# Attention products cut by query columns, and the value sums copied out of PSUM in one piece, in a transformer block on one core

## The chip, the cores and the metric

The kernel runs on one core of one Trainium2 chip. The metric is the device time of one execution in microseconds (us); several executions are timed and their median is given. One more execution is profiled, and everything that is said of single instructions comes from that one.

## What is computed

The input is x, 2048 tokens of 512 numbers. Cut to what matters, the reference is

```python
xn = layernorm(x)
q, k, v = split_heads(xn @ w_qkv.T)          # 16 heads of 32
scores = (q @ k.T) / sqrt(32)                # causal: later keys are masked
attn = softmax(scores) @ v
out = x + attn @ w_o.T + ffn(xn)             # ffn: gated GELU, 4096 wide, 4-bit weights
```

Everything is computed in 32-bit floats. The feed-forward weights are decoded from 4-bit codes in the kernel. The change lies in the attention alone.

## The kernel before

**Stages.** Three stages follow each other. The first (0 to 188 us) normalizes the tokens, makes the values v and the queries and keys of the first four heads, and takes the row maxima of the first two head pairs. The second (188 to 748 us) is the loop at L560 over six head pairs p = 0 to 5; a third part of the attention (748 to 875 us, L655) does the last two pairs together. Then come the output projection and the feed-forward network, to 2002 us.

**One step of the loop.** A pass over one head pair p has 40 steps, written out in `steps` (L191). The queries are taken in blocks `qb` of 512 in the order 1, 2, 3, 0 (ORDER, L71), and for each block the keys in tiles `kt` of 128, from 0 to 4·qb+3. The last four tiles of a block are the diagonal ones, whose first columns are masked away, so that they are 512, 384, 256 and 128 queries wide. This gives steps 0 to 7 for block 1, 8 to 19 for block 2, 20 to 35 for block 3 and 36 to 39 for block 0. A step does, in program order:

- on TensorE two products L281 (one for each head, h = 0 and 1) that put the negated row maxima into a PSUM bank, two products L210 that make scores of a *later* pair `ahead` for its row maxima, and two products L296 that add this pair's transposed scores to the banks of L281;
- on TensorE what `run_due` (L570) has for this step: products of probabilities with values (L344) and row sums (L355) that earlier steps put off with `later_on` (L553), which says how many steps later they run;
- on ScalarE the exponentials of both heads (L310; on a diagonal tile L316, L318 and L320, and then a select on GpSimd, L325);
- on VectorE the row maxima of the later pair (L234; L229 on the diagonal);
- `keep_attention` (L413), if a block's sums are complete, and then one quarter of a division by the row sums (`normalize_attention`, L430: a reciprocal on VectorE, a product on GpSimd), if any is left and the tile isn't a diagonal one.

Each engine works through its own instructions in this order.

**Four tiles make a group of three.** Of four key tiles off the diagonal, called a *quad* below, the first two go through `attend_pair` (L367): four products of 512 columns, two heads by two tiles, each on 32 of the 128 columns of the TensorE array, so that the four run at the same time. GpSimd adds the probabilities of tiles 0 and 1, and of 2 and 3 (`add_up`, L390), so that row sums need one product for two tiles. The third and the fourth tile go through `attend_with_rows` (L375): two products with values and two with ones, again four at a time. The pair's products run in the step of tile 3, those of the third tile in the next step, and those of the fourth two steps after that. So in four steps three have a whole set of four products and one, that of the tile with kt % 4 == 1, has none. A diagonal tile's products (`attend_diagonal`, L380) run three steps later, those of the last one two steps later, in the same step as those of the one before.

**Buffers.** The score banks of L281/L296 come from a pool of three (ps_t, also used by the transposes L262), those of L210 from another pool of three (ps_s, also used by the projections L166 of later heads, which stand in 16 of the 240 steps). The probabilities have four buffers, one for a step. Value sums and row sums have one PSUM bank each (tags m0 and m1), so the next block's first products must wait until the old sums are copied out.

**Copying out.** The value sums of even and odd tiles stand in different partitions, 0 to 63 and 64 to 127 of the bank `av`; the row sums stand in 64 to 127 of `row`. Before the change:

```python
copies[0](aT[og][qb][half], av[:64])
if p < NP - 2 and qb > 0:
    nc.vector.tensor_tensor(aT[og][qb][half], aT[og][qb][half], av[64:], ALU.add)
copies[1](sums[og, qb][half], row[64:])
```

Both copies are ScalarE's, except for p = 7.

Of the kernel before, what the change touches and what calls it, by code (L numbers as in the profile page):

```python
# [42 lines left out]
ALU = mybir.AluOpType  # L43
# [3 lines left out]
P = 128  # L47
# [3 lines left out]
D = H // HEADS  # L51
NT = S // P
TB = 512
# [3 lines left out]
NP = HEADS // 2  # L57
# [21 lines left out]
def block_kernel(  # L79
# [10 lines left out]
    nc = tc.nc  # L90
# [4 lines left out]
    def turn_tile(i, name, dtype=F32, shape=(P, TB)):  # L95
        return turns.tile(list(shape), dtype, tag=f"turn{i}", name=name)
# [5 lines left out]
    aT = [  # L102
        [late.tile([P, TB], F32, tag=f"aT{og}_{b}", name=f"aT{og}_{b}") for b in range(NTB)]
        for og in range(NOG)
    ]
# [8 lines left out]
    with (  # L114
# [42 lines left out]
        def project(og, b, which, ps=None):  # L157
            for _ in project_halves(og, b, which, ps):
                pass
# [26 lines left out]
        units, steps, first = [], [], {}  # L186
# [80 lines left out]
        def rows_when_due():  # L267
            if due and tick[0] >= due[0][0]:
                rows_from_parts()
            tick[0] += 1  # L270

        def score_cols(p, n, pool):

            qb, kt = steps[n]
            c0 = max(0, kt - 4 * qb) * P
            tiles = []
            for h in range(2):
                first = rows_of(p, h).start
                rows = slice(first, first + 3)
                ps = tile_of(pool, f"ps_t{p}_{n}_{h}")  # L280
                nc.tensor.matmul(  # L281
                    ps[:, c0:],
                    lhsT=ones_h[rows, :],
                    rhs=negs[p // 2, qb][rows, c0:],
                    start=True,
                    stop=False,
                )
                tiles.append(ps)
            return tiles
# [44 lines left out]

        avs, rows, sums = {}, {}, {}

        def add_values(p, n, prob, place, start, stop):

            qb, kt = steps[n]
            c0 = max(0, kt - 4 * qb) * P  # L340
            for h in range(2):
                head = 2 * p + h
                j = 2 * place + h
                nc.tensor.matmul(  # L344
                    avs[p, qb][D * j : D * (j + 1), c0:],
                    lhsT=v[kt // 4][:, kt % 4, D * head : D * (head + 1)],
                    rhs=prob[:, h, c0:],
                    start=start,
                    stop=stop,
                )  # L350

        def add_rows(p, qb, probs, c0, start, stop):

            for h in range(2):
                nc.tensor.matmul(  # L355
                    rows[p, qb][D * (2 + h) : D * (3 + h), c0:],
                    lhsT=ones,
                    rhs=probs[h][:, c0:],
                    start=start,
                    stop=stop,  # L360
                )

        def open_sums(p, qb):
            avs[p, qb] = ps_m.tile([P, TB], F32, tag="m0", name=f"av{p}_{qb}")
            rows[p, qb] = ps_m.tile([P, TB], F32, tag="m1", name=f"rows{p}_{qb}")

        def attend_pair(p, n, prob_a, prob_b):  # L367

            qb, kt = steps[n]
            if kt == 0:  # L370
                open_sums(p, qb)
            add_values(p, n, prob_a, 0, kt == 0, False)
            add_values(p, n + 1, prob_b, 1, kt == 0, kt == 4 * qb - 4)

        def attend_with_rows(p, n, prob, added, start):  # L375

            add_values(p, n, prob, 0, False, False)
            add_rows(p, steps[n][0], added, 0, start, False)

        def attend_diagonal(p, n, prob):  # L380
            qb, kt = steps[n]
            if kt == 0:
                open_sums(p, qb)
            last = kt == 4 * qb + 3
            add_values(p, n, prob, 0, kt == 0, last)
            add_rows(p, qb, [prob[:, h] for h in range(2)], (kt - 4 * qb) * P, kt == 0, last)
            if last:
                full.append((p, qb))

# [9 lines left out]
        def attend(p, n, prob, first, last):  # L399

            qb, kt = steps[n]
            if first:
                avs[p, qb] = ps_m.tile([P, TB], F32, tag=f"m{p % 2}", name=f"av{p}_{qb}")
                rows[p, qb] = avs[p, qb]
            add_values(p, n, prob, 0, first, last)
            c0 = max(0, kt - 4 * qb) * P
            add_rows(p, qb, [prob[:, h] for h in range(2)], c0, first, last)
            if last:
                full.append((p, qb))

# [2 lines left out]
        def keep_attention():  # L413

            p, qb = full.pop(0)
            av, row = avs[p, qb], rows[p, qb]
            og, half = p // 2, slice(64 * (p % 2), 64 * (p % 2 + 1))
            if p % 2 == 0:
                sums[og, qb] = sump.tile([P, TB], F32, tag="sums", name=f"sums{og}_{qb}")
            copies = [nc.scalar.copy] * 2  # L420
            if p == NP - 1:
                copies = [nc.vector.tensor_copy] * 2
            copies[0](aT[og][qb][half], av[:64])
            if p < NP - 2 and qb > 0:
                nc.vector.tensor_tensor(aT[og][qb][half], aT[og][qb][half], av[64:], ALU.add)
            copies[1](sums[og, qb][half], row[64:])
            if p % 2 == 1:
                invert.extend((og, qb, i) for i in range(4))

# [94 lines left out]
        for b in range(NTB):  # L524
            n = first[b]
# [27 lines left out]
        def later_on(wait, f, *args):  # L553
            todo.setdefault(at[0] + wait, []).append((f, args))

        def run_due(m):
            for f, args in todo.pop(m, []):
                f(*args)

        for m in range((NP - 2) * STEPS):  # L560
            p, n = divmod(m, STEPS)
            at[0] = m

            ahead = p + 3 if p % 2 == 0 else p + 1
            og, own = p // 2, m % (2 * STEPS)
            rows_when_due()
            ps = score_cols(p, n, ps_t)
            ps_max = score_rows(ahead, n, ps_s)
            add_scores(p, n, ps)
            run_due(m)  # L570
            prob = exponentials(p, n, ps)
            maxima(ahead, n, ps_max)
            while full:
                keep_attention()
            qb, kt = steps[n]


            if kt >= 4 * qb:
                later_on(2 if kt == 4 * qb + 3 else 3, attend_diagonal, p, n, prob)
            elif kt % 2 == 0:  # L580
                even = prob
            else:
                added = add_up(2 * quads + kt % 4 // 2, even, prob)
                if kt % 4 == 1:
                    later_on(2, attend_pair, p, n - 1, even, prob)
                    added_first = added
                else:
                    later_on(1, attend_with_rows, p, n - 1, even, added_first, kt == 3)
                    later_on(3, attend_with_rows, p, n, prob, added, False)
                    quads += 1  # L590
            if invert and kt < 4 * qb:
                normalize_attention()

            if own in places and og + 2 < NOG:
                b, which = places[own]
                project(og + 2, b, which, tile_of(ps_s, f"ps_qk{og + 2}_{b}_{which}"))
            if own in places_own and og > 0 and og + 1 < NOG:
                b, which = places_own[own]
                project(og + 1, b, which, tile_of(ps_s, f"ps_qk{og + 1}_{b}_{which}"))
            if og + 2 < NOG and own == 20:  # L600
                wqk[og + 2] = load_qk(og + 2)
            if og + 2 == NOG and own == max(places_own) + 1:

                wo = []
                for i in range(0, NOG, 2):
                    t = wa.tile([P, 2, H], F32, tag="wqk", name=f"wo{i}")
                    for k in range(2):
                        nc.sync.dma_start(out=t[:, k], in_=w_o[i + k])
                        wo.append(t[:, k])
# [45 lines left out]
        for s, n in enumerate(together):  # L655
# [6 lines left out]
            while pending:  # L662
                attend(*pending.pop(0))
            qb = steps[n][0]
# [4 lines left out]
            for i in range(2):  # L669
                prob = exponentials_together(NP - 2 + i, n, two[i])  # L670
# [135 lines left out]
    for n in range(NG * NC):  # L806
        g, j = divmod(n + 1, NC)
        pieces += [(g, 0, j), (g, 1, j)] if g < NG else [None, None]
        g, j = divmod(2 * (n // 2 + 1) + n % 2, NC)
# [48 lines left out]
    with tc.manual_schedule():  # L858
# [13 lines left out]
        for n, t in enumerate(order):  # L872
            po = bank(f"po{t}")
            for og in range(NOG):
# [3 lines left out]
                    rhs=wo[og],  # L878
                    start=(og == 0),
                    stop=(og == NOG - 1),  # L880
# [187 lines left out]
```

## Time and profile before

| | us |
|---|---|
| median of 3 runs (2004.05 to 2007.36) | 2006.99 |
| profiled execution, its own time | 2004.01 |
| its span, from the first to the last instruction | 2002.3 |
| the loop at L560, within the span | 188.1 to 747.8 |
| reciprocal L434 (VectorE, 128x128), mean of 40 in the loop | 0.944 |
| copies L423 and L426 (ScalarE, 64x512), mean of 23 each in the loop | 0.575, 0.582 |
| addition L425 (VectorE, 64x512), mean of 18 | 0.691 |

Times of single instructions are from start to end; the next instruction of the same engine can begin a little before the end. One product of 32-bit floats is two records in the trace. In a timeline, each line has the start, the length, engine, line, operation, what it writes and reads, the shape and how many records are merged; in brackets stands how long the engine was idle before it and which instruction ended that. In a table of windows, each line has the stretch and its length, then the busy time of TensorE, of its weight loads (PEld), of VectorE (DVE), ScalarE (ACT) and GpSimd (POOL), each with a count of instructions, then the granted TensorE clock as a share, and the DMA share and rate.

### The profile page before, as it was taken

How to read it: one execution, taken by the hardware profiler on the slowest of the kernel's cores; microseconds unless marked ns; L12 is line 12 of the kernel's file. 1: busy time of each engine (PE TensorE's matmuls, PEld its weight loads, DVE VectorE, ACT ScalarE, POOL GpSimd, SP SyncE). 2: the span in 40 equal slices, each digit the busy share in tenths (PEclk: the TensorE clock that was granted, in tenths of full speed). 3: DMA queues.
4: the chain of work that ended last, by engine and by line, in shares of the span. 5: the costliest groups of instructions: out<-in, count | busy, mean ns of one | idle time of the engine just before them, and what ended most of it. 6: DMA issues, size and time to landing. Idle time of an engine off the chain costs nothing.

```text
span 2002.3 us, 30630 instructions
## 1 busy us (share of the span) xinstructions
PE 1931.5 (96%) x10784; PEld 1165.7 (58%) x10784; DVE 1323.6 (66%) x2700; ACT 1107.8 (55%) x2305; POOL 907.6 (45%) x1037
## 2 busy tenths in 40 slices
PE   7999999999999999999999999999999999999998
PEld 3433232333333322236888888888888888888886
DVE  5657665646564666267777777777767676767674
ACT  2112664646455656644666666666666666666664
POOL 1001544445444444144555555555555555555551
PEclk9999999999999999999999999999999999999999
DMA  3000000000000000120000000000000000000002
GB/s 126 0 11 11 1 1 1 1 12 1 1 1 12 1 2 1 36 73 19 22 23 18 23 18 23 18 23 18 23 18 23 18 23 19 22 19 22 19 5 84
DMA packets 55386, 39.77 MB, mean 20 GB/s; under 512 B 14784, under 2 KB 47552, under 8 KB 55232
## 3 DMA queue, kind: packets, MB, share of 16 engines
q1 hardware_dynamic: 55232, 37.81, 6.4%
q8 instruction: 85, 1.39, 0.3%
q14 instruction: 69, 0.57, 0.1%
HBM read 33.55 MB, written 4.19 MB: 19 GB/s over the span
## 4 chain that ended last, share of the span: by engine, by line
PE 94%; ACT 4%; DVE 1%; issue 1%; DMA 0%; DVEq 0%; ACTq 0%
PE gu L920 24%; PE gu L933 12%; PE pd L983 12%; PE av L344 11%; PE ps_s L210 9%; PE pd L995 6%; PE ps_qk L166 6%; PE ps_t L281 4%; PE ps_t L296 3%; PE ps_v L505 3%; PE po L875 3%; ACT prob L310 2%; PE pm L262 1%; PE ptx L494 0%; ACT prob L318 0%
## 5 line engine op out<-in xcount | busy, mean ns | idle before, releaser
L920 PE MATMUL gu<-xh,gu 128*128 128x512 f32 x1024 | 403.9, 394 | 0.0
L920 PE MATMUL gu<-lm,gu 128*128 128x512 f32 x1024 | 403.7, 394 | 0.0
L234 DVE TENSOR_REDUCE tops<-ps_s 128x1 f32<-128x512 f32 x384 | 244.3, 684 | 178.3 <-PE ps_s L210 150.3
L1004 DVE SCALAR_TENSOR_TENSOR acc<-pd,acc 128x512 f32<-128x512 f32 x512 | 317.1, 682 | 2.4 <-PE pd L995 2.4
L210 PE MATMUL ps_s<-qk,qk 32*128 32x512 f32 (+3 forms) x1280 | 298.0, 581 | 0.5
L965 POOL TENSOR_TENSOR parts<-inter,hi 128x512 fp32r<-128x512 f32 x128 | 171.5, 1340 | 277.9 <-DVE hi L961 272.7
L310 ACT ACTIVATE prob<-ps_t 128x512 f32<-128x512 f32 x384 | 205.9, 596 | 154.1 <-PE ps_t L296 133.7
L933 PE MATMUL gu<-lm,gu 128*128 128x512 f32 x1024 | 279.6, 395 | 0.0
L957 DVE SCALAR_TENSOR_TENSOR inter<-gu,gate 128x512 f32<-128x512 f32 x128 | 88.5, 692 | 275.1 <-PE gu L933 273.7
L296 PE MATMUL ps_t<-qk,qk 32*128 32x512 f32 (+3 forms) x1280 | 267.3, 542 | 0.0
L990 ACT ACTIVATE pd<-pd 128x512 f32<-128x512 f32 x512 | 263.4, 581 | 1.1 <-PE pd L983 1.1
L983 PE MATMUL pd<-wd,parts 128*128 128x512 f32 x1024 | 259.6, 396 | 0.0
L344 PE MATMUL av<-prob,v 128*32 128x512 f32 (+3 forms) x1280 | 252.0, 554 | 1.3 <-issue 0.7
L927 ACT ACTIVATE gu<-gu 128x512 f32<-128x512 f32 x256 | 148.7, 581 | 187.9 <-PE gu L920 187.8
L395 POOL TENSOR_TENSOR added<-prob,prob 128x512 f32<-128x512 f32 x144 | 180.0, 1272 | 143.3 <-ACT prob L310 142.8
L933 PEld LDWEIGHTS gu<-lm,gu 128*128 128x128 f32 x1024 | 192.0, 188 | 47.1 <-issue 0.2
L920 PEld LDWEIGHTS gu<-lm,gu 128*128 128x128 f32 x1024 | 191.9, 187 | 46.6 <-POOL wd L790 0.2
L983 PEld LDWEIGHTS pd<-wd,parts 128*128 128x128 f32 x1024 | 192.3, 188 | 45.8
L920 PEld LDWEIGHTS gu<-xh,gu 128*128 128x128 f32 x1024 | 192.0, 188 | 45.7 <-ACT wd L789 0.2
L229 DVE CUSTOM_DVE_ANT_0 ps_s<-ps_s,mask_qk 128x128 f32<-128x128 f32 (+3 forms) x256 | 121.0, 517 | 95.7 <-PE ps_t L296 47.7
L964 ACT CAST parts<-hi 128x512 fp32r<-128x512 f32 x128 | 79.7, 623 | 173.1 <-DVE hi L961 171.3
L281 PE MATMUL ps_t<-neg,ones_h 3*128 3x512 bf16 (+3 forms) x640 | 126.2, 353 | 47.6 <-ACT prob L310 28.3
(103 smaller groups left out, 2820.8 us busy)
## 6 DMA issues: line engine op xcount, KB each, us to landing
pk<-packed SPq DMA_DIRECT2D x96, 128.0 KB, 2.2
sc<-scales SPq DMA_DIRECT2D x512, 8.0 KB, 1.6
x<-x SPq DMA_DIRECT2D x16, 256.0 KB, 4.4
acc<-x SPq DMA_DIRECT2D x16, 256.0 KB, 3.7
sc<-scales SPq DMA_DIRECT2D x256, 16.0 KB, 1.7
out<-acc SPq DMA_DIRECT2D x16, 256.0 KB, 2.2
wqk<-w_qk SPq DMA_DIRECT2D x4, 512.0 KB, 3.7
wv<-w_v SPq DMA_DIRECT2D x4, 256.0 KB, 6.8
```

The lines of the kernel that those rows point to most:

```text
L210: nc.tensor.matmul(ps[:, :w], lhsT=qT[p // 2, qb][rows, i * P : (i + 1) * P], rhs=kT[p // 2, c][rows, :w], start=True, stop=True,)
L234: nc.vector.tensor_reduce(top, ps[:, :w], AX.X, ALU.max)
L281: nc.tensor.matmul(ps[:, c0:], lhsT=ones_h[rows, :], rhs=negs[p // 2, qb][rows, c0:], start=True, stop=False,)
L296: nc.tensor.matmul(ps[:, c0:], lhsT=kT[p // 2, kt // 4][rows, (kt % 4) * P : (kt % 4 + 1) * P], rhs=qT[p // 2, qb][rows, c0:], start=False ...
L310: nc.scalar.activation(prob[:, h, :], ps, AF.Exp)
L344: nc.tensor.matmul(avs[p, qb][D * j : D * (j + 1), c0:], lhsT=v[kt // 4][:, kt % 4, D * head : D * (head + 1)], rhs=prob[:, h, c0:], start ...
L395: nc.gpsimd.tensor_tensor(t, prob_a[:, h], prob_b[:, h], ALU.add)
L920: nc.tensor.matmul(ps, lhsT=parts[:, i, k], rhs=mov, start=(k == 0 and i == 0), stop=(k == NK - 1 and i == 1),)
L933: nc.tensor.matmul(ps, lhsT=gu[g, m, j][:, 2, k], rhs=lm[b, k][1], start=False, stop=(k == NK - 1), skip_group_check=True,)
L983: nc.tensor.matmul(po, lhsT=parts[:, part, i * P : (i + 1) * P], rhs=w[:, part], start=(part == 0), stop=(part == 1),)
L990: nc.scalar.activation(po, po, AF.Copy, scale=HIGH_SCALE)
L1004: nc.vector.scalar_tensor_tensor(acc[t], po, SUM_SCALE, acc[t], ALU.mult, ALU.add)
```

## The change

- `add_values` and `add_rows` take a range of query columns, so that a set of four products can be cut.
- The pair's products are cut into 384 columns in the step of tile 3 and 128 columns in the next step. Those of the third tile are cut into 256 columns in the step after tile 3 and 256 in the one after that. Those of the fourth tile are cut into 128 columns two steps after it and 384 three steps after it. So every step has 384 columns of four products.
- The last diagonal tile's products run three steps later instead of two, and so `keep_attention` and what follows it run one step later too.
- In `keep_attention`, for p < 6 and qb > 0, ScalarE copies the whole bank `av` to a tile `both` in SBUF, VectorE copies the row sums, ScalarE copies the half of `both` that has to change partitions to `aT`, and GpSimd adds the other half. For p < 6 and qb = 0 the value sums stay with ScalarE and the row sums go to VectorE. For p = 6 and 7 nothing changes.

The diff:

```diff
@@ -334,28 +334,28 @@
 
         avs, rows, sums = {}, {}, {}
 
-        def add_values(p, n, prob, place, start, stop):
+        def add_values(p, n, prob, place, start, stop, cols=(0, TB)):
 
             qb, kt = steps[n]
-            c0 = max(0, kt - 4 * qb) * P
+            c0, c1 = max(cols[0], (kt - 4 * qb) * P), cols[1]
             for h in range(2):
                 head = 2 * p + h
                 j = 2 * place + h
                 nc.tensor.matmul(
-                    avs[p, qb][D * j : D * (j + 1), c0:],
+                    avs[p, qb][D * j : D * (j + 1), c0:c1],
                     lhsT=v[kt // 4][:, kt % 4, D * head : D * (head + 1)],
-                    rhs=prob[:, h, c0:],
+                    rhs=prob[:, h, c0:c1],
                     start=start,
                     stop=stop,
                 )
 
-        def add_rows(p, qb, probs, c0, start, stop):
+        def add_rows(p, qb, probs, start, stop, c0=0, c1=TB):
 
             for h in range(2):
                 nc.tensor.matmul(
-                    rows[p, qb][D * (2 + h) : D * (3 + h), c0:],
+                    rows[p, qb][D * (2 + h) : D * (3 + h), c0:c1],
                     lhsT=ones,
-                    rhs=probs[h][:, c0:],
+                    rhs=probs[h][:, c0:c1],
                     start=start,
                     stop=stop,
                 )
@@ -364,18 +364,19 @@
             avs[p, qb] = ps_m.tile([P, TB], F32, tag="m0", name=f"av{p}_{qb}")
             rows[p, qb] = ps_m.tile([P, TB], F32, tag="m1", name=f"rows{p}_{qb}")
 
-        def attend_pair(p, n, prob_a, prob_b):
+        def attend_pair(p, n, prob_a, prob_b, c0, c1):
 
             qb, kt = steps[n]
-            if kt == 0:
+            if kt == 0 and c0 == 0:
                 open_sums(p, qb)
-            add_values(p, n, prob_a, 0, kt == 0, False)
-            add_values(p, n + 1, prob_b, 1, kt == 0, kt == 4 * qb - 4)
-
-        def attend_with_rows(p, n, prob, added, start):
-
-            add_values(p, n, prob, 0, False, False)
-            add_rows(p, steps[n][0], added, 0, start, False)
+            add_values(p, n, prob_a, 0, kt == 0 and c0 == 0, False, (c0, c1))
+            last = kt == 4 * qb - 4 and c1 == TB
+            add_values(p, n + 1, prob_b, 1, kt == 0 and c0 == 0, last, (c0, c1))
+
+        def attend_with_rows(p, n, prob, added, start, c0, c1):
+
+            add_values(p, n, prob, 0, False, False, (c0, c1))
+            add_rows(p, steps[n][0], added, start and c0 == 0, False, c0, c1)
 
         def attend_diagonal(p, n, prob):
             qb, kt = steps[n]
@@ -383,7 +384,7 @@
                 open_sums(p, qb)
             last = kt == 4 * qb + 3
             add_values(p, n, prob, 0, kt == 0, last)
-            add_rows(p, qb, [prob[:, h] for h in range(2)], (kt - 4 * qb) * P, kt == 0, last)
+            add_rows(p, qb, [prob[:, h] for h in range(2)], kt == 0, last, (kt - 4 * qb) * P)
             if last:
                 full.append((p, qb))
 
@@ -404,7 +405,7 @@
                 rows[p, qb] = avs[p, qb]
             add_values(p, n, prob, 0, first, last)
             c0 = max(0, kt - 4 * qb) * P
-            add_rows(p, qb, [prob[:, h] for h in range(2)], c0, first, last)
+            add_rows(p, qb, [prob[:, h] for h in range(2)], first, last, c0)
             if last:
                 full.append((p, qb))
 
@@ -417,13 +418,23 @@
             og, half = p // 2, slice(64 * (p % 2), 64 * (p % 2 + 1))
             if p % 2 == 0:
                 sums[og, qb] = sump.tile([P, TB], F32, tag="sums", name=f"sums{og}_{qb}")
-            copies = [nc.scalar.copy] * 2
-            if p == NP - 1:
-                copies = [nc.vector.tensor_copy] * 2
-            copies[0](aT[og][qb][half], av[:64])
-            if p < NP - 2 and qb > 0:
-                nc.vector.tensor_tensor(aT[og][qb][half], aT[og][qb][half], av[64:], ALU.add)
-            copies[1](sums[og, qb][half], row[64:])
+            if p >= NP - 2:
+                copy = nc.vector.tensor_copy if p % 2 else nc.scalar.copy
+                copy(aT[og][qb][half], av[:64])
+                copy(sums[og, qb][half], row[64:])
+            else:
+                if qb == 0:
+                    nc.scalar.copy(aT[og][qb][half], av[:64])
+                else:
+                    both = turn_tile(8 + p % 2, f"both{p}_{qb}")
+                    nc.scalar.copy(both, av)
+                nc.vector.tensor_copy(sums[og, qb][half], row[64:])
+                if qb > 0:
+                    other = slice(64 * (1 - p % 2), 64 * (2 - p % 2))
+                    nc.scalar.copy(aT[og][qb][half], both[other])
+                    nc.gpsimd.tensor_tensor(
+                        aT[og][qb][half], aT[og][qb][half], both[half], ALU.add
+                    )
             if p % 2 == 1:
                 invert.extend((og, qb, i) for i in range(4))
 
@@ -576,17 +587,21 @@
 
 
             if kt >= 4 * qb:
-                later_on(2 if kt == 4 * qb + 3 else 3, attend_diagonal, p, n, prob)
+                later_on(3, attend_diagonal, p, n, prob)
             elif kt % 2 == 0:
                 even = prob
             else:
                 added = add_up(2 * quads + kt % 4 // 2, even, prob)
                 if kt % 4 == 1:
-                    later_on(2, attend_pair, p, n - 1, even, prob)
+                    later_on(2, attend_pair, p, n - 1, even, prob, 0, 3 * P)
+                    later_on(3, attend_pair, p, n - 1, even, prob, 3 * P, TB)
                     added_first = added
                 else:
-                    later_on(1, attend_with_rows, p, n - 1, even, added_first, kt == 3)
-                    later_on(3, attend_with_rows, p, n, prob, added, False)
+                    start = kt == 3
+                    later_on(1, attend_with_rows, p, n - 1, even, added_first, start, 0, 2 * P)
+                    later_on(2, attend_with_rows, p, n - 1, even, added_first, start, 2 * P, TB)
+                    later_on(2, attend_with_rows, p, n, prob, added, False, 0, P)
+                    later_on(3, attend_with_rows, p, n, prob, added, False, P, TB)
                     quads += 1
             if invert and kt < 4 * qb:
                 normalize_attention()
```

## What was predicted before the changed kernel was run

> **What bounds the kernel now.** I read the page first, then a table of windows by stage, then the timeline of a few steps and the waits inside the loop.
>
> ```profile
> PE 1931.5 (96%) x10784; PEld 1165.7 (58%) x10784; DVE 1323.6 (66%) x2700; ACT 1107.8 (55%) x2305; POOL 907.6 (45%) x1037
> ```
>
> TensorE is busy for 96% of the span, so a gain needs either less of its work or less of its idling. The windows tell where it idles:
>
> ```profile
> 188.10:747.80 559.70, 516.18 (x4237) 170.65 (x4236) 331.90 (x754) 320.74 (x808) 262.41 (x406) 0.98 0.01 4
> 875.00:2002.30 1127.30, 1121.55 (x4719) 885.13 (x4717) 819.84 (x1517) 674.29 (x1264) 599.37 (x519) 1.00 0.09 24
> 554.00:557.40 3.40, 1.80 (x33) 0.95 (x29) 2.24 (x6) 3.10 (x12) 0.82 (x2) 1.00 0.00 0
> 557.40:560.80 3.40, 3.40 (x25) 1.32 (x26) 1.29 (x9) 1.41 (x6) 1.50 (x6) 0.50 0.00 0
> ```
>
> The loop loses 43.5 of its 559.7 us; the feed-forward stage loses 5.8 of 1127 and the change doesn't touch it. The last two rows show a second loss: after 3.4 us with TensorE busy for only 1.80, the next 3.4 us run at half clock. The loop has eight such windows of 3.41 us. Now one quad (block 3, pair 2):
>
> ```profile
> 440.81 0.39 PE L281 MATMUL ps_t<-neg,ones_h 3*128 3x512 bf16 x2
> ...
> 442.98 0.39 PE L281 MATMUL ps_t<-neg,ones_h 3*128 3x512 bf16 x2
> ...
> 444.32 1.09 ACT L310 ACTIVATE prob<-ps_t 128x512 f32<-128x512 f32 x2 [1.09 <-PE ps_t L296]
> 444.97 0.37 PE L281 MATMUL ps_t<-neg,ones_h 3*128 3x512 bf16 x1 [0.53 <-ACT prob L310]
> ```
>
> The step at 440.81 spends 1.18 us on scores (its L344 begins at 441.99 in the same timeline) and 1.00 on its four products. The step at 442.98 has none, so the next starts at 444.07; but its second L281 needs a third bank, which the exponential of head 0 frees only at 444.97, 1.99 after 442.98. So 1.99 us is the least length of a full-width step, and a step without products runs into it. The quad takes 2.18 + 1.09 + 3.06 + 2.18 = 8.50, of which 0.88 is this wait. The end of block 3 shows the other kind of stall:
>
> ```profile
> 554.20 0.41 PE L344 MATMUL av<-prob,v 128*32 128x256 f32 x2
> ...
> 554.66 0.28 PE L344 MATMUL av<-prob,v 128*32 128x128 f32 x2
> ...
> 554.99 0.28 PE L281 MATMUL ps_t<-neg,ones_h 3*128 3x256 bf16 x2
> ...
> 555.66 0.58 ACT L423 COPY aT<-av 64x512 f32<-64x512 f32 x1
> ...
> 556.26 0.58 ACT L426 COPY sums<-rows 64x512 f32<-64x512 f32 x1
> ...
> 557.37 0.25 PE L281 MATMUL ps_t<-neg,ones_h 3*128 3x128 bf16 x1 [1.60 <-ACT prob L318]
> ```
>
> Two copies of ScalarE stand ahead of exponentials for which TensorE waits 1.60 us. VectorE waits too:
>
> ```profile
> PE ps_t L281 <- ACT prob L310: 25.2, 38, 1.2
> PEld ps_s L210 <- DVE aT L425: 23.4, 16, 1.6
> ```
>
> In 16 cases the addition L425, itself 10.9 us behind L423, holds up the row maxima behind it and so the banks of L210. These rows overlap; I count from step lengths instead.
>
> **Cost of the cuts.** From the fence above, four products of 256 columns take 554.66 − 554.20 = 0.46, and 128 columns 0.33 where scores follow: 0.22 for 128 columns, and some 0.11 once where the array goes back to scores. Four of 384 columns take 0.785 (in the step at 419.93: 421.11 to 421.90). So a quad's pieces cost what the whole did, and only one more return to scores, with 0.09 on the way in (1.18 instead of 1.09): four steps of 1.18 + 0.785 = 7.85 against an unstalled 7.62. The Trainium skill speaks against such cuts: "TensorEngine Tiling (Array Packing)", section "Instruction Overhead", gives each matmul some 60 cycles of overhead. A quad has 12 more products, 36 quads 432, each two records. Taken as a fixed addition of 25 ns to each record (an estimate: 60 cycles at 2.4 GHz, the clock in "TensorE: Matmul & The Clock Gate"), that would be 864 × 0.025 = 21.6 us. The rows show no such addition: the 128-column pieces follow each other 0.11 apart (554.66, then 554.77 in the same timeline), half of 0.22. I take 0, and keep 0 to +18 us (four run side by side, so not all adds up).
>
> **Inner quads** (18: one in block 2, two in block 3, six passes). Four steps cannot be shorter than 4 × 1.99 = 7.96. One new wait comes on top. The pair's last 128 columns now read the probabilities of tile 0 in the very step whose exponentials overwrite that buffer; in the changed program's order these wait for TensorE past the scores. The exponential starts 1.34 into the step today (444.32); then 1.18 + 0.11 + 0.27 (end of the second record) + 0.10 = 1.66. Behind it stand head 1's exponential, and the next step's second L281, 0.3 later. Low end 0 if the wait ends with the first product, high 0.5. So 8.23 against 8.50: −0.27, ×18 = −5.
>
> **Diagonal quads of blocks 1 to 3** (18): now 2.18 + 0.82 + 2.46 + 1.44 = 6.90; then 1.96 + 0.23 (the same wait, behind a 0.28 clip) + 1.71 + 1.43 + 1.44 = 6.77. Two hold projections that already cover their stall and lose 0.6 each: together −1.
>
> **Starts of blocks.** The last diagonal products, and with them `keep_attention` with its copies, addition and first reciprocal, move one step later: past one step's exponentials on ScalarE, maxima on VectorE, and a select or add on GpSimd; no DMA moves. ScalarE still makes two copies: the bank's, 0.58 as for a 128x512 L180 (0.586), and one out of SBUF, nearest row L423's 0.58 (bounds 0.5 to 0.62, L964's). VectorE exchanges L425 (0.69) for a copy (0.68, its L423 row), which waits for TensorE alone; six blocks 0 add such a copy, under steps of 2 us with 1.3 of VectorE work. GpSimd gains 18 additions of 64x512: 0.46 (L436) to 1.27 (L395); I take 1.27, together 23 us on an engine busy 262 of 560.
> Counted from the second L281 of step kt = 0, with 1.96 to 1.99 for each step, those of kt = 1, 2, 3 come at 1.99, 3.95 and 5.91. ScalarE ends the exponentials of kt = 2 at 6.24 (5.26, and twice 0.49, their distance in the timeline), the bank's copy at 6.84, the second at 7.48. The pair that opens the freed bank is ready at 5.91 + 1.16 = 7.07: no wait, at most 0.5. The exponentials of kt = 3 start at 7.5 instead of 7.22, and the transposes L262 take the third bank, so kt = 4 has its second L281 at 8.64.
> GpSimd's addition, behind the second copy, ends at 8.8, a product with reciprocals (0.46) at 9.3, and the two adds of tiles 2 and 3 queued behind them at 11.8. The fourth tile's first piece, now a step earlier than before, wants them in step 5, at 10.9 + 1.18 + 0.44 = 12.5. Slack 0.7, so nothing, high end +10.
> So four steps of blocks 1 to 3, today 8.74 (1.96 + 1.98 + 1.09 + 3.71), become 8.64 without reciprocals: −0.1, 17 times, −1.7. With reciprocals they are 0.9 to 1.4 longer today. After, VectorE needs 1.3 + 0.95 a step against 1.98, 0.27 too much in each of up to four steps, of which a spare bank hides about half: 0.6 longer. Eight blocks (both later blocks of pairs 1, 3, 5, one of pairs 2 and 4) win 0.3 to 0.8, in all −4.8.
> For block 0 in step 36 to 39: today 1.96 + 1.71 + 0.56 + 3.79 = 8.02 (odd pairs), 7.82 (even). After, step 37 frees its bank 1.66 after its start (554.51 + 0.38 today) at 1.96 + 1.66 = 3.62, and the exponentials of step 38, with no copies ahead, free theirs at 4.78 instead of 6.05. Head 1 and L320 last to 5.2, the bank's copy to 5.85; only then the diagonal products of block 0 open the sums (today no wait there), 1.0 + 0.33 for L262: end at 7.16. −0.86 and −0.66, three each: −4.6.
>
> **Half clock.** The same step takes 6.43 with such a window and 4.84 without (step 23 in pairs 3 and 1), block 0 9.41 and 8.02: the eight cost 11.1. "TensorE: Matmul & The Clock Gate", section "The HAM clock gate", says that the clock halves after an idle window of some 3.4 us and that windows run freely. By "idle" taken strictly none of these would have come: the rows show 1.80 of 3.40 busy before. The measurement decides: a thin window suffices. The stalls of 1.6 us go and every step gets products, so I expect two of eight to stay: −8.3 (bounds 0 and −11).
>
> **Sum**: 5 + 1 + 1.7 + 4.8 + 4.6 + 8.3 = 25 off the profiled execution's 2004.0 gives 1979. The median stood 3.0 above that execution; since half-clock windows come and go, I put a third of it on top: 1980.
>
> **Rivals.**
> - *Stalls shrink, the clock windows stay as many*: −17, 1989. For: windows run freely, new gaps are made at bank `av`. Against: the thin windows all lie in stalls that shrink. 0.13.
> - *More is won* (no wait at the buffers, no half clock): −5 − 3 − 6 more, 1966. 0.06.
> - *Each piece costs its overhead after all*: −25 + 18, 1999. Against: the 0.11. 0.08.
> - *It doesn't do what it says*: the exponentials behind the pair's last piece pass on the whole stall (36 steps × 0.7 more), so steps are even and as slow: 2005. 0.05.
> - *Slower*: GpSimd's addition waits for two ScalarE copies and holds the adds behind it, and 18 times the fourth tile's first piece waits. The 25 won are gone when each is 1.4 beyond the slack of 0.7; with 3 us lateness (3 − 0.7 − 1.4) × 18 = +16: 2022. For: the sums are wanted a step sooner, in-order queue. Against: GpSimd idles half of the loop. 0.06.
>
> The forecast has 0.62. Faster (0.62 + 0.13 + 0.06 + 0.08) 0.89, within 0.2% 0.05, slower 0.06; 0.2% is about what a measurement of this kernel can tell from no change. The range 1966 to 1998 takes in the forecast's own 1970 to 1990, the clock rival, and stops short of the overhead one.
>
> **What would show it.** Full-width steps of 1.96 to 2.0 us, the kt % 4 == 0 step followed by a wait of 0.3 on L310; 128-column pieces 0.11 apart; block 0 ending near 7.2; at most three windows at 0.50; no wait of L210 for the copy of the sums; L355 waiting for L395 nowhere by more than 0.3. If L355 waits for L395 at block starts, or L281's waits sum to more than 35 us, the forecast is wrong.

## The result and the profile after

The changed kernel takes 1975.38 us (median of 6, 1972.27 to 1975.79) against 2005.52 before (median of 6, 1999.39 to 2007.36): a ratio of 0.985, 95% interval 0.9833 to 0.9866. The profiled execution took 1972.27 with a span of 1970.2; forecast were 1979 for it and 1980 for the median.

The table of windows by stage shows where the 32.1 us of span went: 31.2 in the loop, 0.7 in the last two pairs, 0.1 each ahead of the loop and behind those pairs.

```profile
188.00:716.50 528.50, 520.14 (x5105) 188.21 (x5105) 334.11 (x759) 318.12 (x803) 281.70 (x419) 1.00 0.02 4
843.00:1970.20 1127.20, 1121.48 (x4718) 885.03 (x4717) 819.93 (x1517) 673.89 (x1264) 598.93 (x519) 1.00 0.09 24
```

The loop's clock went from 0.98 to 1.00: in this execution not one half-clock window is left in it, of eight. TensorE's idle time, as the profile counts it, fell from 43.5 to 8.4 us. The waits inside the loop changed their names:

```profile
ACT prob L310 <- PE av L344: 23.3, 18, 1.4
...
PEld ps_s L210 <- DVE tops L234: 11.9, 33, 1.2
...
PE av L344 <- ACT both L430: 4.2, 6, 0.7
...
PE ps_t L281 <- ACT prob L310: 2.3, 3, 1.2
```

L281's wait for L310 fell from 25.2 to 2.3, the wait behind the sums' addition on VectorE (23.4) is gone, and two that the prediction had named are new: exponentials behind L344, and the products that open a block's sums behind the copy of the bank (in block 0 alone). The first is seen in an inner quad (block 3, pair 2), from the timeline:

```profile
431.52 1.09 ACT L310 ACTIVATE prob<-ps_t 128x512 f32<-128x512 f32 x2 [1.24 <-PE av L344]
...
431.79 0.75 PE L281 MATMUL ps_t<-neg,ones_h 3*128 3x512 bf16 x2
...
433.33 0.41 PE L344 MATMUL av<-prob,v 128*32 128x256 f32 x2
...
433.79 0.28 PE L344 MATMUL av<-prob,v 128*32 128x128 f32 x2
...
433.90 0.28 PE L344 MATMUL av<-prob,v 128*32 128x128 f32 x2
...
434.12 0.39 PE L281 MATMUL ps_t<-neg,ones_h 3*128 3x512 bf16 x2
```

This exponential belongs to the step that began at 429.81; it starts 1.71 into it (forecast 1.66, before 1.34). The two L281 at 431.79 are merged into one line of 0.75 where a step without a wait has 0.39: the second came 0.36 late. That step has 2.33 us, the other three 1.97 each. The profile counts TensorE as busy over the gap, because the first product's modelled end covers it; only the distance of the starts shows this wait. The falls above are therefore too large: taken over all 240 steps, the second L281 starts 64.4 us after the first before the change and 35.5 after it, where the lists of waits for L310 and L318 show 43.0 and 2.5. The pieces of 128 columns are 0.11 apart (433.79, 433.90), as predicted. The end of block 0 in the same pair:

```profile
449.95 0.43 ACT L320 ACTIVATE prob<-clip 128x256 f32<-128x256 f32 x1
...
450.27 0.59 ACT L430 COPY both<-av 128x512 f32<-128x512 f32 x1
...
451.00 0.62 PE L344 MATMUL av<-prob,v 128*32 128x512 f32 x2 [0.70 <-ACT both L430]
```

Where TensorE waited 1.60 us for exponentials behind two copies, it now waits 0.70 behind the bank's one copy.

The largest term, the starts of blocks, is seen at block 2 of pair 5, a start with reciprocals. Before:

```profile
683.00 0.69 DVE L425 TENSOR_TENSOR aT<-aT,av 64x512 f32<-64x512 f32 x1 [0.58 <-ACT aT L423]
...
683.72 0.95 DVE L434 RECIPROCAL sums<-sums 128x128 f32<-128x128 f32 x1
...
684.25 0.29 PEld L210 LDWEIGHTS ps_s<-qk,qk 32*128 32x128 f32 x2 [1.57 <-DVE aT L425]
...
684.71 1.29 DVE L234 TENSOR_REDUCE tops<-ps_s 128x1 f32<-128x512 f32 x2
```

After:

```profile
659.59 0.69 DVE L431 COPY sums<-rows 64x512 f32<-64x512 f32 x1
...
660.01 0.62 ACT L434 COPY aT<-both 64x512 f32<-64x512 f32 x1
...
660.32 0.95 DVE L445 RECIPROCAL sums<-sums 128x128 f32<-128x128 f32 x1
660.65 1.08 ACT L310 ACTIVATE prob<-ps_t 128x512 f32<-128x512 f32 x2
660.77 1.26 POOL L435 TENSOR_TENSOR aT<-aT,both 64x512 f32<-64x512 f32 x1 [1.15 <-ACT aT L434]
```

Before, VectorE waits 0.58 us for ScalarE's first copy and then works through addition and reciprocal ahead of the maxima that free L210's banks. After, its copy needs no other engine's copy, and the four steps of this start take 8.63 us instead of 9.87.

### The profile page after: what moved, and what is told of

The parts are those of the page before. It is cut to its first block, busy times and chain, and to the rows that moved or that the text cites. A ratio compares the mean times of both kernels' runs of the same rounds, so it can differ in the third digit from the quotient of the medians.

```text
span 1970.2 us, 32411 instructions
## 1 busy us (share of the span) xinstructions
PE 1934.5 (98%) x11648; PEld 1182.9 (60%) x11648; DVE 1326.7 (67%) x2706; ACT 1104.2 (56%) x2299; POOL 927.6 (47%) x1055
## 4 chain that ended last, share of the span: by engine, by line
PE 94%; ACT 3%; POOL 1%; issue 1%; DVE 1%; DMA 0%; DVEq 0%; ACTq 0%; POOLq 0%
PE gu L935 24%; PE gu L948 12%; PE pd L998 12%; PE av L344 10%; PE ps_s L210 8%; PE pd L1010 6%; PE ps_qk L166 6%; PE ps_t L281 4%; PE ps_t L296 3%; PE ps_v L516 3%; PE po L890 3%; ACT prob L310 2%; POOL added L396 1%; PE ptx L505 0%; PE pm L262 0%
## 5 line engine op out<-in xcount | busy, mean ns | idle before, releaser
L310 ACT ACTIVATE prob<-ps_t 128x512 f32<-128x512 f32 x384 | 205.7, 596 | 145.6 <-PE ps_t L296 102.1
L210 PE MATMUL ps_s<-qk,qk 32*128 32x512 f32 (+3 forms) x1280 | 286.4, 576 | 0.0
L344 PE MATMUL av<-prob,v 128*32 128x128 f32 (+3 forms) x1856 | 257.6, 425 | 5.5 <-ACT both L430 4.2
L344 PEld LDWEIGHTS av<-prob,v 128*32 128x32 f32 x1856 | 67.2, 108 | 206.2 <-issue 147.5
```

The costliest lines, as they stand in the source:

```text
L210: nc.tensor.matmul(ps[:, :w], lhsT=qT[p // 2, qb][rows, i * P : (i + 1) * P], rhs=kT[p // 2, c][rows, :w], start=True, stop=True,)
L310: nc.scalar.activation(prob[:, h, :], ps, AF.Exp)
L344: nc.tensor.matmul(avs[p, qb][D * j : D * (j + 1), c0:c1], lhsT=v[kt // 4][:, kt % 4, D * head : D * (head + 1)], rhs=prob[:, h, c0:c1], s ...
```

## The experiments

Each time is set against the kernel before as measured beside it, whose median was 2003.39, 2004.58, 2004.34 or 2007.07. Differences to the changed kernel (1975.38) compare measurements made apart, and 1 or 2 us of them are not told from zero. Lengths are from one second L281 to another, as in the prediction. Nine of the twelve profiles below have a half-clock stretch of 3.4 or 6.8 us near 193 us, at the first start; the profiles of before and after have none there. This stretch and the first start are left out of the counts and lengths below. The theory: the gain comes from three places, the starts of blocks, the half clock that their stalls bring about, and, for a small part, the even steps. The rival: the cuts, which the change is named after, carry it.

### The three parts, alone and in pairs

Cuts alone: the changed kernel with this line of before, and the old `keep_attention`.

```diff
-                later_on(3, attend_diagonal, p, n, prob)
+                later_on(2 if kt == 4 * qb + 3 else 3, attend_diagonal, p, n, prob)
```

> The kernel before with the products cut by columns as in the change, but with the old copies and the last diagonal products still two steps late. Theory (most of the gain comes from the starts of blocks and from the half clock, a smaller part from even steps): inner quads go from 8.50 to 8.23 as in the changed kernel, starts of blocks keep their stalls on L423, L425 and L426 and win only the smaller pair (0.2 each), half-clock windows stay at four or more: 3 to 15 us below before, likeliest 8. Rival (the cuts alone carry the gain): 20 us or more below before.

Measured: 1998.27, 5.1 below before, ratio 0.997 (0.9959 to 0.9982). Undisturbed inner quads take 8.23 to 8.24 us, but starts still 8.74 and 9.87, where 0.2 less was expected. Seven half-clock windows stay, and so does the wait at block starts:

```profile
PEld ps_s L210 <- DVE aT L426: 23.3, 16, 1.6
```

The rival falls.

Copies alone: the kernel before with the new `keep_attention`.

> The kernel before with the new keep_attention alone. Theory: VectorE no longer waits for L423, so starts of blocks with reciprocals lose some 0.5 of their 0.9 to 1.4 extra, the others 0.1; the short steps stay, inner quads stay at 8.50: 2 to 14 us below before, likeliest 6, with some half-clock windows left. Rival (the copies carry most of it): over 18 us below. Rival (another copy on ScalarE's queue costs): no gain.

Measured: 1991.15, 12.2 below, ratio 0.9937 (0.9925 to 0.995), twice the likeliest, inside what was expected. Starts with reciprocals take 9.3 instead of 9.9, inner quads 8.50 or 8.44, and two windows are left of eight.

Delay alone: the kernel before with `later_on(3, attend_diagonal, ...)`.

> The kernel before with the last diagonal products, and so the old copies, one step later; nothing is cut and the copies are the old ones. Theory: ScalarE's copies no longer stand ahead of the exponentials of tile 2, but the bank of the value sums now comes free only after L425, some 0.5 after the pair wants it; the two about cancel: between 8 us below and 4 us above before, likeliest 2 below; block 0 wins some 0.3 each. Rival (the place of the copies in ScalarE's queue is what counts): 12 us or more below.

Measured: 1994.43, 9.0 below, ratio 0.9949 (0.9937 to 0.9961): outside what was expected. Starts without reciprocals did get slower, 8.91 instead of 8.74, for the reason given: TensorE now waits for the bank.

```profile
PE av L344 <- DVE aT L425: 15.0, 18, 1.6
```

Block 0 takes 8.17 to 8.33 instead of 7.82 to 8.02, where a gain of 0.3 was expected. But starts with reciprocals fell from 9.87 to 9.05 (the wait of L210 behind L425 is gone), and half-clock windows from eight to one. The theory had left both out.

Cuts and delay, with the old copies:

> The changed kernel with the old keep_attention (ScalarE copies the first half, VectorE adds the second half from PSUM, ScalarE copies the row sums). Theory: the bank is free after L425 instead of after one copy, 0.5 to 0.7 late at each of 18 block starts, and the maxima are late behind it: 8 to 16 us slower than the changed kernel, that is some 20 below before. Rival (the copies are off the path once the steps are even): within 3 us of the changed kernel.

Measured: 1991.92, 11.5 below before, 16.5 above the changed kernel, just outside what was expected, ratio to before 0.9941 (0.9928 to 0.9953). The same 15.0 us of wait stand behind the addition. Block 0 takes 8.17 to 9.41 instead of 7.48, and three half-clock stretches are back, one of them two windows long.

Cuts and copies, without the delay:

> The changed kernel with the last diagonal products two steps late again, as before: only the delay is undone. Theory (the delay takes the copies from ahead of tile 2's exponentials and gives the step of tile 2 its products): the step of tile 2 has no products, so tile 3's waits 0.1 to 0.3 for L310 again, and block 0 has its copies ahead of step 38's exponentials; no VectorE wait behind L423: 3 to 10 us slower than the changed kernel, likeliest 6, with one to four half-clock windows. Rival (the delay is worth nothing once the rest is done): within 2 us of the changed kernel.

Measured: 1983.61, 20.7 below before, 8.2 above the changed kernel, ratio 0.9896 (0.988 to 0.9912). Starts with reciprocals take 9.2 to 9.6 instead of 8.5 to 8.9, those without 8.37 to 8.50 as in the changed kernel; block 0 takes 7.59 to 7.73, hardly more than 7.48, so there the delay is worth little. No window comes back, where one to four were expected.

Copies and delay, without the cuts:

> The changed kernel without the cuts: new copies and the delay, but whole sets of products in three of four steps as before. Theory: inner quads take 8.50 instead of 8.23 (18), starts of blocks some 0.2 more for the whole pair (17), diagonal quads 6.89 instead of 6.78, half-clock windows stay near none since the long waits are gone: 6 to 12 us slower than the changed kernel, likeliest 9. Rival (the cuts carry the gain): 18 us or more slower. Rival (they are worth nothing beside the other two parts): within 3 us.

Measured: 1980.05, 27.0 below before, 4.7 above the changed kernel, ratio 0.9872 (0.9855 to 0.9888). Less than expected: the starts of blocks 2 and 3 take 8.49 and 8.63, as with cuts, and no window comes back. The inner quads take 8.43 to 8.59 instead of 8.23 to 8.40, and the loop 5.5 us more (533.96 against 528.44, neither with a half-clock window). So of the 30 us the cuts carry some 5, whether they are made first or last. Copies and delay together carry the rest, 27.0, which is more than the 12.2 and 9.0 of each alone.

### What the half clock costs, and what it takes

The kernel before with idle work where TensorE waits, `FILL = {3: 14, 11: 14, 23: 14, 39: 24}` by step:

```diff
+                if h == 0 and p < NP - 2 and n in FILL:
+                    for _ in range(FILL[n]):
+                        nc.tensor.matmul(ps[:, :P], lhsT=ones_h, rhs=ones_h, start=True, stop=True)
```

> The kernel before with idle work added: in steps 3, 11 and 23 of each pass 14, in step 39 24 products of ones by ones (128 columns, bf16) into the bank that the first L281 then overwrites, at the place where TensorE waits 1.1 to 1.8 us. Nothing else changes. Theory (thin windows make the half clock): the added work hides in the waits, at most three half-clock windows of eight are left, and the time falls by 6 to 11 us. Rival (the windows have another cause): eight windows, time unchanged or up to 5 us longer.

Measured: 1993.94, 10.6 below before, ratio 0.9942 (0.9928 to 0.9956), by added work alone. Every start but the first and every block 0 takes what the undisturbed ones of before took (for instance 8.74, 9.87, 8.02, 7.82), so nothing else moved. No window is left but one near 193 us.

The same, with 3 rows of the array in each product instead of 128 (`lhsT=ones_h[rows, :], rhs=ones_h[rows, :]`):

> As the run with idle work in the waits of steps 3, 11, 23 and 39 (14 and 24 products of 128 columns, bf16), but each on 3 of the 128 rows of the array, as L281's products are, instead of all 128. Theory A (TensorE's busy time decides about the clock): the same as with whole-array products, at most three windows, 8 to 11 us below before. Theory B (the share of the array that is at work counts): five or more windows stay and less than 5 us is won.

Measured: 2004.53, ratio 0.9999 (0.9989 to 1.0008), and eight windows. The groups of the idle products (first the 128-row kernel, then the 3-row one) show the same count and busy time:

```profile
L284 PE MATMUL ps_t<-ones_h 128*128 128x128 bf16 x396 | 26.7, 222 | 0.0
```

```profile
L284 PE MATMUL ps_t<-ones_h 3*128 3x128 bf16 x396 | 26.7, 217 | 0.0
```

and the loop's window rows, in the same order, differ in clock and length:

```profile
188.10:737.40 549.30, 528.77 (x4630) 190.22 (x4628) 332.06 (x757) 319.98 (x808) 261.26 (x404) 1.00 0.01 4
```

```profile
188.10:750.30 562.20, 540.03 (x4630) 194.56 (x4628) 331.74 (x756) 320.76 (x808) 261.63 (x404) 0.97 0.01 4
```

In the 3-row kernel TensorE was busy for 3.15 to 3.30 of the 3.41 us ahead of each of the eight windows (before: 1.81 to 2.69), and half clock followed all the same. Two neighbouring rows:

```profile
561.82:565.23 3.41, 3.15 (x52) 2.42 (x52) 2.48 (x11) 3.14 (x12) 0.81 (x2) 1.00 0.00 0
565.23:568.64 3.41, 3.41 (x22) 1.09 (x14) 0.21 (x2) 1.14 (x3) 1.42 (x6) 0.50 0.00 0
```

Theory B holds as far as it was tried: TensorE's busy time does not decide about the clock; products on all 128 rows keep it up, as many on 3 rows do not. Numbers of rows between them were not tried.

### The prices of single terms

Pieces of 128 columns throughout: each set is made in a loop `for c in range(c0, c1, P)`.

> The changed kernel with every cut set of products cut further into pieces of 128 columns: 864 more products, 1728 more records. Theory (pieces cost their columns): within 2 us of the changed kernel. Rival (each record has a fixed cost of 25 ns): 43 us slower if they add up, 11 us if the four that run side by side share it.

Measured: 1974.20 (ratio to before 0.9841, 0.9826 to 0.9857), within 2 us of the changed kernel with 864 more products. Its loop takes 528.94 us against 528.44, neither with a half-clock window: 0.5 more, where 25 ns a record would make 11 to 43. From its timeline, within one step:

```profile
433.25 0.28 PE L344 MATMUL av<-prob,v 128*32 128x128 f32 x2
...
433.36 0.28 PE L344 MATMUL av<-prob,v 128*32 128x128 f32 x2
...
433.47 0.28 PE L344 MATMUL av<-prob,v 128*32 128x128 f32 x2
```

Every 0.11 us one set of records of 128 columns, as in larger pieces. The overhead rival is refuted for these shapes.

Five buffers of probabilities: `probs` from 4 to 5, paid for with `sums` from 5 to 4 and `tops` from 6 to 5.

> The changed kernel with five buffers of probabilities instead of four (paid for by four instead of five row-sum buffers and five instead of six of the maxima), so that exponentials never wait for the pair's last piece. Theory: the step after a kt % 4 == 0 step goes from 2.33 to 1.97 in inner quads (16 not hidden by projections) and from 1.96 to 1.71 in diagonal ones (15): 9 us faster than the changed kernel, 40 below before. Rival (the wait only moves to the three score banks): at most 3 us faster.

Measured: 1966.62, ratio to before 0.9807 (0.9791 to 0.9823), 8.8 below the changed kernel. The same inner quad in its timeline:

```profile
427.17 0.39 PE L281 MATMUL ps_t<-neg,ones_h 3*128 3x512 bf16 x2
...
429.13 0.40 PE L281 MATMUL ps_t<-neg,ones_h 3*128 3x512 bf16 x2
...
431.11 0.39 PE L281 MATMUL ps_t<-neg,ones_h 3*128 3x512 bf16 x2
...
433.08 0.39 PE L281 MATMUL ps_t<-neg,ones_h 3*128 3x512 bf16 x2
```

All steps of this quad take 1.96 to 1.98, the quad 7.88, the diagonal quads 6.53 instead of 6.78. The new wait was the one at the probability buffer, and its price was right.

GpSimd's addition twice, the second into a spare tile (`nc.gpsimd.tensor_tensor(spare[half], both[half], both[half], ALU.add)`):

> The changed kernel with a second GpSimd addition of 64x512 right behind L435, into a spare tile that nobody reads: GpSimd is 1.26 us later at 18 block starts. Theory: the sums of tiles 2 and 3 have 0.9 (with reciprocals) to 1.2 us to spare, so 0 to 0.4 of it is felt: 0 to 6 us slower than the changed kernel. Rival (GpSimd is on the path already): 18 x 1.26 = 22 us slower.

Measured: 1976.60, ratio to before 0.9852 (0.9832 to 0.9873), 1.2 above the changed kernel. Only quads after a start with reciprocals got longer, 8.59 instead of 8.40 for instance, and all inner quads together 1.3 us. GpSimd has nearly all of its 18 × 1.26 us to spare.

Last, five buffers and idle work (20, 12 and 12 products) in steps 1 to 3 of the first pass:

> The kernel with five buffers of probabilities, with idle whole-array products (20, 12 and 12 of 128 columns, bf16) in steps 1, 2 and 3 of the first pass, where TensorE waits 0.9 to 1.6 us and a half-clock window at 193 us costs 2.7 to 3.0 in some executions. Theory: the window goes, the time is 1 to 3 us below the one with five buffers and its two levels (some 3 apart) become one: 1964 to 1966. Rival (the window comes from the stage before): no gain.

Measured: 1963.84 (1963.48 to 1964.67), ratio to before 0.9796 (0.9783 to 0.9809): the fastest version, 11.5 below the changed kernel and 2.8 below the one with five buffers alone. No half-clock window is left in its loop, the one near 193 us included.

## Why the prediction was right, point by point

The measured column sets the changed kernel's lengths against those of the kernel before with whole-array idle work, which has no half-clock window but the one near 193 us, where it costs the first start 1.7 us (10.62 against 8.93); this is taken out and the clock is counted apart.

| term | forecast, us | measured, us |
|---|---|---|
| inner quads | −5 | −4.1 (189.33 to 185.24) |
| diagonal quads | −1 | 0.0 (144.81 to 144.81) |
| starts of blocks (17) | −6.5 | −12.3 (157.0 to 144.7) |
| block 0 | −4.6 | −2.7 (47.51 to 44.86) |
| half clock | −8.3 | −12.1 (559.7 to 549.3 − 1.7) |
| sum in the loop | −25.4 | −31.3, with 0.1 in the first start |

The total came closer than its parts: starts and half clock gave 9.6 us more than forecast, quads and block 0 gave 3.8 less. That these misses partly cancel is luck.

- **Cuts**: right. Inner quads take 8.23 as forecast; the 0.9 missing in the sum are in the main the quads behind starts with reciprocals (8.40). The overhead that spoke against them was rightly set aside for these shapes. The Trainium skill ("TensorEngine Tiling (Array Packing)", section "Instruction Overhead") also says that a product of one column takes as long as one of 60: a least length, and no addition to longer ones. The runs agree: 864 products on top lengthened the loop by 0.5 us.
- **The new wait at the buffer**: right, mechanism and size: 0.36 measured, 0.3 forecast; a fifth buffer gives 8.8 us back. The sign that L281's waits stay under 35 us was ill chosen: the list shows 2.5 and the distances of the starts 35.5, because the list cannot see this wait.
- **Diagonal quads**: −0.1 each as forecast (6.90 to 6.78), but the two of block 1 with projections lose 1.08 each (13.43 to 14.51) instead of 0.6, so the sum is 0 instead of −1. The 0.6 is what they lose with cuts alone (14.04); copies and delay together add 0.4 (13.83 without cuts), and why is not shown.
- **Starts of blocks**: the mechanism is right and the term mis-sized, by half; the eight with reciprocals won 9.7 instead of 5.6 (0.1 each and 4.8). Without reciprocals they take 8.49, not 8.64: counted from the start, ScalarE's copy out of SBUF ended at 7.47 as worked out (7.48), but the exponentials of kt = 3 began at 7.38, before its record ended. With reciprocals they take 0.14 more, and the quad behind them 0.17, together 0.3 instead of 0.6. With five buffers, where the buffer's wait is gone, it is 0.14 and 0.28: the two waits overlap in part, and 0.6 was too much besides.
- **Block 0**: mechanism right, 7.48 instead of 7.16. Each link of ScalarE's chain came 0.1 to 0.2 later than counted: the bank's copy ended 6.00 after the start, not 5.85, and the products behind it began at 6.15.
- **Half clock**: the step "I expect two of eight to stay" was too cautious; none did in the profiled execution, and the eight had cost 12.1 us rather than 11.1. With no window left, the rival of unchanged windows is refuted; the idle-work run shows what they cost alone, 10.6 us in the median. The reason given, "a thin window suffices", was right, but the quantity was not: it counted busy time, and the 3-row run had half clock behind windows that were 92% to 97% busy.
- **GpSimd's lateness**, the rival for a slower kernel: the addition took the 1.26 us assumed (1.27). Doubling it cost some 1.3 us in all instead of (1.26 − 0.7) × 18 = 10, so its slack was larger than the 0.7 that was worked out.

## What to carry to other kernels

A copy or an addition that stands ahead of the bottleneck's feeder in a queue can stall the bottleneck; to move it one step back in the queue, or to the engine that needn't wait for another, won more here (27 us) than making the bottleneck's own steps even (5 us). When work is cut so that it spreads over steps, ask which buffer the later piece keeps alive: here one more buffer was worth 9 us on top. Look at the starts of products, not only at lists of waits. And read the clock with the waits: here eight windows at half clock cost 12.1 us, some 1.5 each, nearly as much again as the stall of 1.60 us that stands ahead of one of them.

## What the runs showed of the hardware

- 396 idle bf16 products of 128x128 in waits took 10.6 us off the kernel before and removed all eight half-clock windows of its profile; as many with 3 rows of the array, just as long on TensorE (26.7 us), took nothing off and left eight. In this kernel the windows follow how many rows the idle work uses and not TensorE's busy time.
- A half-clock stretch of 6.8 us near 193 us makes the first start 11.3 to 12.1 us long instead of 8.8 to 9.0, one of 3.4 us makes it 10.6. Idle work there removed it: all four executions of that version lie within 1.2 us. The executions of the changed kernel are 1972.27, 1972.29 and four from 1975.08 to 1975.79. That such a stretch makes the difference is likely but not shown: the longer ones were not profiled, and the version with pieces of 128 columns took 1974.44 in its profiled execution without such a stretch, 2.2 us more than the changed kernel's, 1.7 of them ahead of the loop.
- Pieces of four 32-column f32 products follow each other at 0.11 us for 128 columns in each of their two records; 864 more products in such pieces lengthened the loop by 0.5 us.
